# Keeping the last group's image in SBUF, from the adds of layer 2 to the output of layer 3

## The chip, the cores and the metric

The kernel runs on one core of one Trainium2 chip. The metric is device time in microseconds of that core, from the first to the last instruction of one execution, with what lies around it; the median of several executions is compared. Engines are named as in the profile: PE (TensorE), DVE (VectorE), ACT (ScalarE), POOL (GpSimd), SP (SyncE, which issues nearly all DMAs).

## What is computed

The input is 16 images of 32 channels of 128 x 128 in float32. Four layers follow each other, each of the form `x = x + f(groupnorm(x))`, where the norm runs over two channels of one image:

```python
x = x + _L0_conv_ref(_gn(x), W2, b2, W1, b1)     # recurrent layer, along one axis
x = x + _L1_conv_ref(_gn(x), weight)             # 8-bit adder layer, sums of |patch - w|
x = x + _L2_conv_ref(_gn(x), weights1)           # Hartley transform, 32 x 32 modes mixed
x = x + _L3_conv_ref(_gn(x), ...)                # five edge filters, then an encoder and decoder
```

The change lies in layers 2 and 3. Layer 3 applies five edge filters, normalises each filter's result, and runs conv1, pooling, conv2, pooling, conv3, pooling, conv4, and then three pairs of a 2 x 2 transposed convolution and a 3 x 3 convolution (deconv1 and conv5, deconv2 and conv6, deconv3 and conv7). Its result is `orig * y`, where `orig` is the normalised x, and the kernel's output is x plus that.

## The kernel before

`program` runs layer 0 (`stage0`), and then `rest` runs everything else. The 16 images are four groups of four; an image's 32 channels take one quarter of the 128 partitions, so that a group fills them (image, channel).

**Order of the work.** In `rest` the adder layer (`Differences.run`, L757, L760, L647) goes through the images one after the other. Beside it a generator, `After.work`, does layers 2 and 3 for groups 0 to 2 whose images are finished. It yields estimates of its PE work and of waits, and the class `Weave` uses these to decide after which adder instructions its steps are written down; a step that has to come later is put off with `weave.later(us, step)`. When the adder layer is over, group 2 is half done, and a copy of the generator, `end`, does group 3. `drain` then merges the two by their estimated clocks, and from there on only this order, and the compiler's own ordering of what is ready, sets each engine's queue. When group 2 is over, `weave.alone` is set, group 3 uses eight PSUM banks where it had four, and evictions alternate between DVE and ACT.

**Group 3's stages**, which are those of any group:

- `forward`: the transform, and the mixing of the modes.
- `back` (L1254 on): the mixed modes go back through two products (L1278, L1323). `residual` loads pieces of x2, the input of this layer, in 16 DMAs (L1257, 512 KB each), eight ahead. For each piece `take_out` adds the product to it (L1301) and takes `bn_stats` (L1303). The sum, x3, is stored to DRAM (L1307), after which the buffer is loaded again. Then the norm's mean and scale are worked out (`stats3`, `shift3` at L1341).
- `frames` (L1346 on): a ring of four buffers `xp` of 20 rows each, which is 16 rows and a halo of two rows above and below; a buffer has 132 columns. Half a buffer at a time, x3 is loaded (L1367, up to 640 KB), normalised in place by ACT (L1373) with its mirrored border columns copied (L1379, L1380), and stored to DRAM as `xn` with its borders (L1392).
- `statistics`: the mean and variance of the five filters' results, from products of every image row with itself and the next two (L1428), summed with tables on DVE (L1492). Behind the ring, later pieces are loaded 2 us, and normalised 18 us, after a half has been read; at the end the ring is filled again from `xn` (L1397).
- The filters are folded into conv1's 5 x 5 weights `wf` (L1557, L1559) and border terms (L1719), and `conv1` (L1745) reads the ring, which is again loaded from `xn`. conv2 follows.
- `small_layers`: conv3, conv4 (L1595), and the pairs up5 and up6. A pair of transposed convolution and convolution is one set of 2 x 2 products for each of the four positions in an output cell (`Composed.round`, L905, with border terms at L930). After up6, `spread` writes each 32 partitions of PSUM apart (L1683 on DVE, L1686 on ACT) into y6, an image of 66 x 66 for each (image, channel).
- `last`: the pair up7 in 16 rounds, eight pairs of them, four units of 32 rows. Here PSUM's partitions are (quarter of the unit's rows, output channel) and the bank is the image. xr is loaded from `xn` in that layout (16 DMAs of 528 KB, L1814; group 3 has buffers for all four units). The means and scales are brought to this layout by a product (L1826), each pair of rounds is taken out by four DVE operations (L1874, `(acc + one) * v`), and each unit gets four ACT operations that add the mean (L1844) and 16 stores of 128 KB (L1853).

Of the kernel before, what the change touches and what calls it, by code (L numbers as in the profile page):

```python
# [7 lines left out]
F32 = mybir.dt.float32  # L8
# [8 lines left out]
HW = H * W  # L17
# [475 lines left out]
def rest(nc, tc, cst, sel16, bias, m1, r1, a, d, out):  # L493


    with ExitStack() as ctx:
        sm = ctx.enter_context(tc.tile_pool(name="s1_sm", bufs=1))
        stat = sm.tile([128, B, 8, 6], F32, name="stat2")
        with tc.tile_pool(name="s1_ps0", bufs=2, space=PSUM) as ps:
            first = Differences(nc, sm, ps, cst, sel16, m1, r1, a["adder_w"], d, stat)  # L500
        bg = ctx.enter_context(tc.tile_pool(name="b_ps", bufs=4, space=PSUM))
        after = After(nc, tc, "left", sm, bg, cst, bias, a, d, stat, out)
        weave = after.weave = Weave(after.work(range(NG - 1)))
        start = len(nc.cur_bb.bb.instructions)
        with ExitStack() as front:
            first.run(tc, front, weave)
        keep_order(nc, tc, start)

        end = copy.copy(after)
        end.side, end.ps = "right", ctx.enter_context(tc.tile_pool(name="c_ps", bufs=4, space=PSUM))  # L510
        end.spare = bg

        end.buffers = {"t_x": 8, "xm": 8, "xw": 4, "t_w": 6, "t_r": 8, "frames": 4, "gm": 5, "e_v": 6, "l_x": 4}
        end.weave = Weave(end.work([NG - 1]))
        end.weave.now = end.weave.base = weave.now
        end.weave.finished = B - 1
        drain(weave, end.weave)
# [315 lines left out]
class Composed:  # L833
# [59 lines left out]

    def round(self, src, n, acc, pick):

# [3 lines left out]
        for tap in range(4):  # L899
            for j in range(4):  # L900
                par, row, rows, o = pick(j)
                top, left = row + par // 2 + tap // 2, par % 2 + tap % 2
                for blk in range(4):
                    part = slice(32 * blk, 32 * blk + 32)
                    nc.tensor.matmul(  # L905
                        acc[blk][32 * j : 32 * j + 32, o : o + rows * n],
                        t[part, 4 * par + tap, :],
                        src[part, top : top + rows, left : left + n],
                        start=tap == 0,
                        stop=tap == 3,  # L910
                        skip_group_check=True,
                    )
            yield rows * n / 512 * 0.2 + 0.95
            if tap != 2:
                continue
            for j in range(4):
                par, row, rows, o = pick(j)
                pr, pc = par // 2, par % 2
# [7 lines left out]
                for k, to, width in parts:  # L926
                    for blk in range(4):
                        part = slice(32 * blk, 32 * blk + 32)
                        b = self.bd[part]
                        nc.tensor.matmul(  # L930
                            acc[blk][32 * j : 32 * j + 32, to],
                            t[part, 16 + k, :],
                            bass.AP(b.tensor, b.offset, [list(b.ap[0]), [0, width]]),
                            start=False,
                            stop=False,
                            skip_group_check=True,
                        )
# [21 lines left out]
class After:  # L959


    def __init__(self, nc, tc, side, sm, ps, cst, bias, a, d, stat, out):
        self.nc, self.tc, self.side, self.ps, self.cst, self.bias = nc, tc, side, ps, cst, bias
        self.a, self.d, self.stat, self.out = a, d, stat, out
        self.spare, self.banks = None, 0
        self.sm, self.scales = sm, {}
# [9 lines left out]
    def work(self, groups):  # L976
        if 0 in groups:
            yield from self.prepare()
        for g in groups:
            with self.pool("g_sm") as sm:  # L980
# [6 lines left out]
                with ExitStack() as kept:  # L987
                    yield from self.encoder(g, kept)
                    yield from self.last(g, g + 1 if g + 1 in groups else None)

# [250 lines left out]
    def back(self, g, load):  # L1241
# [6 lines left out]
        with self.pool("t_z") as zp_, self.pool("t_r", ahead) as rp:  # L1248
# [6 lines left out]
            def residual(n):  # L1255
                xr.append(rp.tile([128, 2, 4 * W], F32, name="xr2"))
                nc.sync.dma_start(xr[n], rows(n)(x2))  # L1257

            xr = []
            stat = zp_.tile([128, 32, 6], F32, name="stat3")  # L1260
            zi = zp_.tile([128, 32, 32], F32, name="zi")
            for blk in range(4):
# [3 lines left out]
                )  # L1266
            for n in range(ahead):
                residual(n)
            yield -12.0
# [26 lines left out]
            def take_out(n, pf):  # L1296
                while ready.get(n):
                    weave.done(ready[n])
                for r in range(2):
                    v = xr[n][:, r]  # L1300
                    nc.vector.scalar_tensor_tensor(v, pf[r], 2.0**-15, v, ALU.mult, ALU.add)  # L1301
                for r in range(2):
                    nc.vector.bn_stats(stat[:, 2 * n + r, :], xr[n][:, r])  # L1303
                weave.dve += 2.8

                def store():
# [29 lines left out]
            take_out(*previous)  # L1336
            weave.later(7.0, lambda: [load(ch, half) for ch in range(self.buffers["frames"]) for half in range(2)])
            mv = zp_.tile([128, 1, 2], F32, name="mv3")
# [4 lines left out]
            )  # L1343
            yield -2.5

    def frames(self, g, pool):  # L1346
# [54 lines left out]
    def statistics(self, g, pool, frames, sides, out, tables):  # L1401
# [9 lines left out]
        ahead = self.buffers["frames"]  # L1411
        ready = {(n // 2, n % 2): normalise(n // 2, n % 2, 0.5 + 4.0 * n) for n in range(2 * ahead)}
        tables_ahead = self.buffers["gm"]
# [23 lines left out]
        for ch in range(H // 16):  # L1437
# [3 lines left out]
            for l in range(2, 18):  # L1441
                if l == 8:
                    yield ("done", ready[ch, 1])
                    store(ch, 1)
                r = 16 * ch + l - 2
                own = [r2 for r2 in (r, r + 1) if (r, r2) in GRAM_AT]
# [16 lines left out]
                if (ch, half) in ((0, 0), (H // 16 - 1, 1)):  # L1463
# [3 lines left out]
                    for k, cols in enumerate(ends):  # L1467
                        nc.vector.tensor_copy(c[:, :, 2 * k : 2 * k + 2], xp[:, rows, cols])
                weave.dve += 0.3

                def following(ch=ch, half=half):
# [45 lines left out]
    def encoder(self, g, kept):  # L1517


        nc, tc, cst, weave, bias = self.nc, self.tc, self.cst, self.weave, self.bias  # L1520
        y2 = self.padded(kept.enter_context(self.pool("e_y2")), 32, "y2")
        with self.pool("e_in") as xp:
            frames = self.frames(g, xp)
            yield from self.back(g, frames[0])
            with self.pool("e_f") as fp:
                yield from self.first_layers(g, fp, frames, y2)
# [44 lines left out]
    def small_layers(self, cp, rp, y1, y2):  # L1571
# [3 lines left out]
        if not y1:  # L1575
# [3 lines left out]
            y3, y4, y5 = (self.padded(cp, n, f"y{i}") for n, i in ((16, 3), (16, 4), (32, 5)))  # L1579
            self.y6 = y6 = self.padded(rp, 64, "y6")  # L1580
            yield -7.0
# [48 lines left out]
        def upsampled(src, n, up, dst):  # L1630

            rows = min(n, 512 // n)
            for r in range(0, n, rows):
# [15 lines left out]
                yield -2.0 if n == 16 else -4.5  # L1649

        if y1:
            yield from conv(y1, 64, "conv2", pool_into(y2, 64, 1))
            return
        yield from conv(y2, 32, "conv3", pool_into(y3, 32, 2))
        yield from conv(y3, 16, "conv4", flat)
        yield from upsampled(y4, 16, up5, y5)
        yield from upsampled(y5, 32, up6, y6)

# [17 lines left out]
    def spread(self, dst, src, blk, b, engine):  # L1676

        nc, weave = self.nc, self.weave
        for j in range(4):
# [5 lines left out]
            else:  # L1685
                nc.scalar.activation(d, s, AF.Identity, bias=bj)  # L1686
                weave.act += 0.45

    def conv1(self, g, pool, frames, y1, sides, wf, b1):
# [107 lines left out]
        for v in spreads:  # L1797
            weave.done(v)

    def last(self, g, following_group):  # L1800
# [252 lines left out]
```

## Time and profile before

| what | us |
|---|---|
| median of 3 runs (lowest, highest) | 6654.82 (6647.18, 6657.32) |
| the profiled execution | 6630.3 |
| its span, first to last instruction | 6628.4 |
| PE busy, DVE busy, ACT busy | 5329.5, 5552.5, 5436.8 |
| DMA read and written in HBM | 510.69 MB and 200.00 MB |
| largest group: ACT d_act, L757 | 4428.8 in 626 instructions |
| second: DVE d_dve, L760 | 3871.9 in 1678 |
| the chain that ended last, by engine | PE 32%, issue 29%, DVE 20%, ACT 14%, DMA 3% |

A profile line of a group names the line of the kernel, the engine, the operation, what it writes and reads with shapes, the count, busy us and mean ns, and the idle time of the engine ahead of it with what ended it. "issue" is idle time for which the profile shows no wait. A busy PE is not a PE at its peak, since matmuls overlap; therefore the prediction also looks at how many of them a stretch holds. The granted clock is a share of the full TensorE clock.

### The profile page before, as it was taken

The page shows a single profiled execution, that of the slowest core. Times are in us where ns is not written, and L with a number is a line of the kernel's source. Part 1 is how long each engine was busy: PE and PEld are TensorE (multiplying, and loading weights), DVE is VectorE, ACT ScalarE, POOL GpSimd, SP SyncE. Part 2 cuts the span into 40 slices and gives each one's busy share as a digit, 9 for nine tenths or more (in the row PEclk, how much of TensorE's full clock was granted, in tenths as well). Part 3 has the DMA queues.
Part 4 walks back from the last instruction along what each step waited for, and adds up shares of the span by engine and source line. Part 5 has one row for each costly group of instructions (what it writes and reads, how often), then busy time and mean ns, then how long its engine had stood idle before and what let it go on. Part 6 is the DMA issues. An engine that isn't in the chain of part 4 may idle for free.

```text
span 6628.4 us, 269240 instructions
## 1 busy us (share of the span) xinstructions
PE 5329.5 (80%) x126168; PEld 2776.6 (42%) x126168; DVE 5552.5 (84%) x6858; ACT 5436.8 (82%) x3191; POOL 69.9 (1%) x67
## 2 busy tenths in 40 slices
PE   3698677787777879997887879998877879887896
PEld 3676233333334433333333433333333433454584
DVE  7898899999999989998999999999999998242322
ACT  3898899999999999998999989999999998102112
POOL 0000000000000000000000000000000000000000
PEclk9999899999988989998989889999998889988897
DMA  7553322121254632212553732221553642347304
GB/s 317 213 189 116 79 55 62 53 53 45 67 146 114 196 92 72 57 45 52 123 150 97 216 110 61 56 55 43 133 147 90 196 122 76 115 136 216 94 27 108
DMA packets 380767, 728.06 MB, mean 110 GB/s; under 512 B 73284, under 2 KB 225348, under 8 KB 368772
## 3 DMA queue, kind: packets, MB, share of 16 engines
q1 hardware_dynamic: 372180, 676.41, 35.7%
q0 software_dynamic: 7040, 33.80, 1.5%
q8 instruction: 987, 16.17, 1.0%
q14 instruction: 128, 1.05, 0.1%
q10 hardware_dynamic: 432, 0.64, 0.0%
HBM read 510.69 MB, written 200.00 MB: 107 GB/s over the span
## 4 chain that ended last, share of the span: by engine, by line
PE 32%; issue 29%; DVE 20%; ACT 14%; DMA 3%; SPq 1%; POOL 0%; DVEq 0%; ACTq 0%; POOLq 0%
DVE d_dve L760 12%; PE acc L1745 11%; ACT d_act L757 10%; PE acc L647 9%; PE pg L223 3%; PE acc L905 3%; PE acc L1595 2%; PE acc L1428 2%; ACT gt L237 2%; DVE y L1683 1%; ACT junk L198 1%; DVE stat L124 1%; DMA x_in<-in_x_dram 1%; ACT th L247 1%; DVE pooled L1672 1%
## 5 line engine op out<-in xcount | busy, mean ns | idle before, releaser
L757 ACT ACTIVATE d_act<-q,neg 128x8192 f16<-128x8192 f16 (+1 forms) x626 | 4428.8, 7151 | 152.5 <-PE acc L647 125.7
L760 DVE TENSOR_SCALAR d_dve<-q,qw 128x8192 f16<-128x8192 f16 (+1 forms) x1678 | 3871.9, 2362 | 168.8 <-PE acc L647 149.2
L647 PE MATMUL acc<-d_dve,sel 128*32 128x512 f16 x26848 | 1873.4, 402 | 441.7 <-DVE d_dve L760 375.9
L647 PEld LDWEIGHTS <-sel 128*32 128x32 f16 x36864 | 1002.0, 100 | 2084.2 <-issue 1413.5
L1745 PE MATMUL acc<-xp,wf 32*32 32x512 f32 x25600 | 971.3, 607 | 19.0 <-issue 15.6
L647 PE MATMUL acc<-d_act,sel 128*32 128x512 f16 x10016 | 727.2, 412 | 311.5 <-ACT d_act L757 298.4
L1745 PEld LDWEIGHTS acc<-xp,wf 32*32 32x32 f32 x25600 | 420.9, 103 | 368.9 <-issue 287.5
L1686 ACT ACTIVATE y<-pooled,b 32x128 f32<-32x128 f32 x456 | 182.3, 400 | 427.8 <-DVE pooled L1672 421.7
L677 PE MATMUL acc<-q,zero 128*32 128x512 f16 x5676 | 406.5, 398 | 0.8 <-issue 0.8
L905 PE MATMUL acc<-y,u_conv 32*32 32x256 f32 (+1 forms) x9728 | 342.4, 469 | 77.3 <-issue 59.5
L223 PE MATMUL pg<-h,wb 64*64 64x20 f32 (+15 forms) x8192 | 342.4, 306 | 59.4 <-DVE h L251 33.0
L237 ACT ACTIVATE gt<-pg,bias 128x20 f32<-128x20 f32 (+15 forms) x1024 | 332.5, 384 | 41.5 <-PE pg L223 39.3
L223 PEld LDWEIGHTS pg<-h,wb 64*64 64x64 f32 x8192 | 252.5, 151 | 133.9 <-DVE h L251 79.5
L1428 PE MATMUL acc<-xp 32*64 32x204 f32 (+3 forms) x8576 | 252.9, 345 | 62.0 <-issue 61.7
L905 PEld LDWEIGHTS acc<-y,u_conv 32*32 32x32 f32 x9728 | 155.1, 111 | 205.0 <-issue 158.0
L1844 ACT ACTIVATE xr<-xr,l_ms 128x1024 f32<-128x1024 f32 x64 | 68.8, 1147 | 208.7 <-DVE xr L1874 158.8
L1428 PEld LDWEIGHTS acc<-xp 32*64 32x64 f32 (+1 forms) x8576 | 172.1, 134 | 152.9 <-issue 147.0
L677 PEld LDWEIGHTS <-zero 128*32 128x32 f16 x5676 | 169.4, 101 | 156.0 <-issue 30.5
L1780 DVE TENSOR_TENSOR acc<-acc,cut 128x4 f32<-128x4 f32 x256 | 36.3, 165 | 233.0 <-PE acc L1745 230.4
L1373 ACT ACTIVATE xp<-xp,shift,stats 128x1280 f32<-128x1280 f32 (+1 forms) x64 | 91.4, 1433 | 162.6 <-DVE shift L1341 111.6
L1874 DVE SCALAR_TENSOR_TENSOR xr<-acc,l_one,xr 128x512 f32<-128x512 f32 x128 | 87.6, 743 | 155.0 <-PE acc L905 134.7
L223 PE MATMUL pg<-xn,wb 64*64 64x2 f32 (+63 forms) x4096 | 185.5, 291 | 27.1 <-issue 18.8
(217 smaller groups left out, 3748.1 us busy)
## 6 DMA issues: line engine op xcount, KB each, us to landing
q<-q_d SPq DMA_DIRECT2D x128, 536.2 KB, 9.8
xp<-xn_d SPq DMA_DIRECT2D x64, 660.0 KB, 5.0
xp<-x_d SPq DMA_DIRECT2D x56, 640.0 KB, 6.4
xr<-xn_d SPq DMA_DIRECT2D x64, 528.0 KB, 11.9
x_in<-in_x_dram SPq DMA_DIRECT2D x16, 2048.0 KB, 14.7
xn<-in_xs_dram SPq DMA_DIRECT2D x64, 512.0 KB, 7.1
res<-in_x_dram SPq DMA_DIRECT2D x64, 512.0 KB, 8.9
x_d<-res SPq DMA_DIRECT2D x64, 512.0 KB, 5.1
```

The source lines that it names most:

```text
L223: nc.tensor.matmul(bank[c][q][64 * pair : 64 * pair + 64, :, :width], wb[half, 4 * kind + KIND[q]].rearrange("p b o -> p (b o)"), v[half], ...
L237: nc.scalar.activation(gt[:, q, :, :n], bank[c][q][:, :, :n], AF.Tanh if q == G else AF.Sigmoid, bias=bias[:, KIND[q] : KIND[q] + 1],)
L647: self.nc.tensor.matmul(acc[k][32 * j : 32 * j + 32, :], self.sel16[:, i // 9, :], d[:, row : row + 4, c : c + W], start=first, stop=last,)
L677: self.nc.tensor.matmul(acc[k][32 * j : 32 * j + 32, :], self.zero, q[:, :4, :W], start=False, stop=False)
L757: nc.scalar.activation(dst, src, AF.Relu, bias=self.neg[:, i : i + 1])
L760: nc.vector.tensor_scalar(dst, src, self.qw[:, i : i + 1], 0.0, ALU.subtract, ALU.max)
L905: nc.tensor.matmul(acc[blk][32 * j : 32 * j + 32, o : o + rows * n], t[part, 4 * par + tap, :], src[part, top : top + rows, left : left + ...
L1373: nc.scalar.activation(v, v, AF.Identity, bias=self.shift3, scale=self.stats3[:, 1])
L1428: nc.tensor.matmul(gram[blk][j : j + width, at : at + n], xp[part, l, 2 + j : 2 + j + width], xp[part, rows, j : j + width + 4], start=sta ...
L1595: nc.tensor.matmul(acc[blk][32 * j : 32 * j + 32, : rows * n], wc[name][part, tap, :], src[part, at : at + rows, kw : kw + n], start=tap == 0,
L1686: nc.scalar.activation(d, s, AF.Identity, bias=bj)
L1745: nc.tensor.matmul(acc[blk][32 * j : 32 * j + 32, :], tap_of("all", tap)[rows], xp[rows, 4 * j + kh : 4 * j + kh + 4, kw : kw + W], start= ...
```

## The change

Only group 3 takes the new way (`end.whole = True`); groups 0 to 2 keep the old one.

- One tile `image` of 128 x 132 x 132 floats is made ahead of `back`. x2 is loaded into it by 16 DMAs of eight rows each, all issued at once. `take_out` adds in it and takes its statistics from it; x3 is neither stored nor loaded.
- All 16 normalising steps work in it, put off by 0.5 + 1.5 n us, and nothing is stored or loaded again; a chunk of 20 rows is a view of it. Ahead of a chunk's row 16 the statistics now wait for the next chunk's first half, since the halo is shared. conv1 reads the same views.
- up6 writes y6 as four quarters of 16 rows with one halo row above and below: the partitions are (quarter, channel), and the image is a free dimension. For this its rounds take all quarters of the rows at once, with half the columns in a product and twice the products; each bank is taken out by one operation of 128 partitions, and six copies fill the halo rows between quarters.
- In the last rounds a bank is therefore a quarter of the rows, and its partitions are (image, channel), as in `image`. up7 is multiplied into `image` in place, the mean is added in place, and four DMAs of 512 KB for each unit store the output. The loads of `xn` and the product for the means are gone.

```diff
-        end.spare = bg
+        end.spare, end.whole = bg, True
...
-    def round(self, src, n, acc, pick):
+    def round(self, src, n, acc, pick, quarter=0):
...
+                    par, row, rows, o = pick(blk if quarter else j)
+                    top, left = row + par // 2 + tap // 2 - quarter * blk, par % 2 + tap % 2
                     part = slice(32 * blk, 32 * blk + 32)
+                    own = src[part, j] if quarter else src[part]
...
+            if self.whole:
+                for row in [32 * i + 8 * k for k in range(4) for i in range(4)]:
+                    src = bass.AP(x2.tensor, x2.offset + g * 4 * CHW + row * W, [[HW, 128], [W, 8], [1, W]])
+                    nc.sync.dma_start(self.image[:, 2 + row : 10 + row, 2 : W + 2], src)
+            else:
+                for n in range(ahead):
+                    residual(n)
...
+                    v, p = xr[n][:, r] if not self.whole else in_place(n, r), pf[r]
+                    if self.whole:
+                        p = p.rearrange("p (r w) -> p r w", w=W)
+                    nc.vector.scalar_tensor_tensor(v, p, 2.0**-15, v, ALU.mult, ALU.add)
...
+                if self.whole:
+                    return
...
+    def kept_image(self, pool):
...
+        self.image = t = pool.tile([128, PW, PW], F32, name="image")
...
+                v = t[:, row : row + 8, 2 : W + 2]
+                nc.scalar.activation(v, v, AF.Identity, bias=self.shift3, scale=self.stats3[:, 1])
...
+                nc.scalar.copy(t[:, lo:hi, 1], t[:, lo:hi, 3])
+                nc.scalar.copy(t[:, lo:hi, W + 2], t[:, lo:hi, W])
...
+        nothing = lambda ch, half: None
+        return nothing, normalise, nothing, nothing, lambda ch: t[:, 16 * ch : 16 * ch + 20, :]
...
+        if self.whole:
+            ready = {(n // 2, n % 2): normalise(n // 2, n % 2, 0.5 + 1.5 * n) for n in range(H // 8)}
...
+                if l == 16 and self.whole and ch + 1 < H // 16:
+                    yield ("done", ready[ch + 1, 0])
...
+        def to_quarters(src, n, up, dst):
...
+            for pr in range(2):
+                acc = [self.acc() for _ in range(4)]
+                for pc in range(2):
+                    yield from up.round(src, n, acc, lambda j: (2 * pr + pc, rows * j, rows, 256 * pc))
+                yield SUMMED
+                for blk in range(4):
+                    self.evict(
...
+            self.neighbours(dst, 2 * rows)
...
-        yield from upsampled(y5, 32, up6, y6)
+        yield from (to_quarters if self.whole else upsampled)(y5, 32, up6, y6)
...
+    def neighbours(self, t, n, above=True, below=True):
...
+        for q in range(3):
+            a, b = t[32 * q : 32 * q + 32], t[32 * q + 32 : 32 * q + 64]
+            if above:
+                self.nc.vector.tensor_copy(b[:, :, 0, 1 : w - 1], a[:, :, n, 1 : w - 1])
+            if below:
+                self.nc.vector.tensor_copy(a[:, :, n + 1, 1 : w - 1], b[:, :, 1, 1 : w - 1])
...
+    def last_in_place(self, g):
...
+            for unit in range(4):
+                for pr in range(2):
+                    acc = [self.acc() for _ in range(4)]
+                    for pc in range(2):
+                        pick = lambda q: (2 * pr + pc, 16 * q + 4 * unit, 4, 256 * pc)
+                        yield from up.round(self.y6, 64, acc, pick, 16)
+                    yield SUMMED
+                    for q in range(4):
+                        first = 2 + 32 * q + 8 * unit + pr
+                        v = x[:, first : first + 7 : 2, 2 : W + 2].rearrange("p r (w b) -> p r w b", b=2)
+                        nc.vector.scalar_tensor_tensor(
+                            v, acc[q].rearrange("p (b r w) -> p r w b", b=2, w=64), one, v, ALU.add, ALU.mult
+                        )
+                    yield -2.5
+                for q in range(4):
+                    row = 32 * q + 8 * unit
+                    v = x[:, 2 + row : 10 + row, 2 : W + 2]
+                    nc.scalar.activation(v, v, AF.Identity, bias=self.stats3[:, 0])
+                    to = self.out.offset + g * 4 * CHW + row * W
+                    nc.sync.dma_start(bass.AP(self.out.tensor, to, [[HW, 128], [W, 8], [1, W]]), v)
```

## The prediction

> **What bounds the kernel now.** I read the page's 40 slices first, to see where the change can act at all.
>
> ```profile
> PE   3698677787777879997887879998877879887896
> DVE  7898899999999989998999999999999998242322
> ACT  3898899999999999998999989999999998102112
> ```
>
> The last line of columns matters: for 34 slices (to about 5640 us) VectorE and ScalarE are full, the adder layer's loop sets the time, and the diff touches nothing there. In the last six slices both are nearly idle: this is the tail, where groups 2 and 3 finish side by side and then group 3 alone. All of the change lies there. Next I asked for the tail stage by stage (columns: stage, length, busy us and counts of PE, weight loads, DVE, ACT, POOL, then granted clock, DMA share, GB/s).
>
> ```profile
> 5868.00:5966.00 98.00, 77.33 (x1750) 49.83 (x1750) 66.93 (x154) 6.39 (x16) 0.00 (x0) 0.71 0.57 175
> 6006.00:6136.00 130.00, 93.26 (x3194) 58.87 (x3193) 17.85 (x48) 24.50 (x37) 0.00 (x0) 0.88 0.73 187
> 6136.00:6204.00 68.00, 39.84 (x1608) 29.06 (x1612) 38.98 (x100) 4.30 (x4) 2.15 (x4) 0.60 0.45 121
> 6204.00:6443.00 239.00, 236.11 (x7482) 183.77 (x7465) 44.69 (x144) 34.21 (x72) 0.00 (x0) 0.98 0.15 44
> 6514.00:6560.00 46.00, 26.34 (x834) 17.22 (x836) 7.83 (x15) 4.08 (x5) 0.00 (x0) 0.58 0.89 184
> 6560.00:6614.00 54.00, 39.30 (x1818) 27.09 (x1791) 13.63 (x20) 10.21 (x10) 0.00 (x0) 0.94 0.50 119
> ```
>
> In order (counts are matmul records, two for each fp32 product): group 3's way back; its statistics beside group 2's last rounds; the folding of conv1's weights; conv1; the first and the second part of group 3's last rounds. Only conv1 is full of TensorE work. The last two rows are the same instructions, yet 834 matmuls took 46 us beside a DMA share of 0.89, and 1818 took 54 us beside 0.50. The PE's order of time in the statistics shows how it loses time (start, us, instructions, idle before):
>
> ```profile
> 6017.02 3.02 PE L1428 MATMUL acc<-xp 32*64 32x204 f32 x128 [0.95 <-issue]
> 6021.03 3.02 PE L1428 MATMUL acc<-xp 32*64 32x204 f32 x128 [1.00 <-issue]
> 6030.54 3.00 PE L1428 MATMUL acc<-xp 32*64 32x204 f32 x57 [6.49 <-issue]
> 6039.85 4.70 PE L1428 MATMUL acc<-xp 32*64 32x204 f32 x128 [3.92 <-issue]
> 6049.36 4.37 PE L1428 MATMUL acc<-xp 32*64 32x204 f32 x91 [4.80 <-issue]
> ```
>
> Runs of 128 matmuls with gaps that no semaphore explains. The page has 17.2 MB on its instruction queues (16.17 and 1.05) for 269240 instructions, 64 B each, and 987 packets on the first, 16.4 KB each: 256 instructions, which are 128 matmuls with their 128 weight loads. So a gap ends when the next packet of instructions lands, and it is 1 us when the DMA engines are quiet and 4 to 6.5 us when they are loaded. I measure by the packet: 130 us for 3194 matmuls are 5.21 us a packet, 54 us for 1818 are 3.80.
>
> Last, the waits of PE over the way back, and of the DMA queue over the last rounds:
>
> ```profile
> PE acc L1595 <- DMA w_conv<-in_conv_dram: 10.8, 1, 10.8
> PE acc L905 <- issue: 3.8, 2, 3.5
> ```
>
> The first is group 2's conv3, whose weights SP could not issue before 5922.25, behind reloads that waited for x3 stores to land.
>
> **The change part by part**, against the profiled execution (6630.3 us, its span 6628.4); lower is a gain.
>
> *Way back (5868 to 5987).* Removed: 16 stores of x3 (L1307, 512 KB), the reloads tied to them, and 16 loads of frames (L1367, 640 KB). The 16 image loads (512 KB) go out at once where now 8 do, at about 5812; at the 250 to 390 GB/s that the loads between 5810 and 5824 show, 8.4 MB take 22 to 34 us, and the first add comes at 5894: hidden; without that cover they would cost some 10 us. conv2's last eviction ends at 5920.1 and conv3 needs it, so conv3 restarts there instead of 5926.2: -6. Between 0 (the adds on DVE set the pace anyway, 67 of 98 us busy) and -11. The adds and bn_stats work on rows 132 apart instead of a solid block; the near row is the strided L1874, 744 ns against 683 for L1301: at most 32 x 0.06 = +2, taken as 0.
>
> *Normalising (ACT).* Sixteen steps of 1024 columns: 1.25 + 2 x 0.21 = 1.67 us, 27 us in all, now 30. They no longer wait for x_d (ACT waited 44.9 us for it). But they become ready together when the shift is ready (5986.5), and up to 9 more of them than now (7) may stand on ACT ahead of group 2's up6 evictions (8 x 0.73 us), for which PE waited 5.1 us already: 0 to +15. PE can take statistics instead, so I take the lower part, +5. The new halo wait (row 16 on the next chunk's first half) queues the remaining statistics behind it on PE; with steps of 1.67 us for 8 rows against 3.8 us of PE a packet (8 rows) it costs 0.
>
> *Statistics beside group 2 (6006 to 6136).* Removed: the store of xn (8.7 MB), the loads of x3 (7 MB) and of xn again (5.3 MB), 21 of the 44.8 MB moved between 5960 and 6210; also their places on SP, which group 2's loads and stores stood behind. The 23.8 MB left, over some 200 us, are 119 GB/s, the very figure of the 3.80 us row. 25.0 packets x (5.21 - 3.80) = -35. [...] Ends: 0, and -43 at 3.47 us a packet (5865.4 to 5868.9, DMA share 0.06).
>
> *Folding (6136 to 6204).* 37 us are DVE's chain (es_w, square root, wf), untouched. PE then idles 13.1 us in the 704 matmuls of L1719, with out stores beside it: -6, between 0 and -13.
>
> *conv1.* 236.1 of 239 busy: -2 (0 to -3).
>
> *up6 and the small layers (6443 to 6514).* up6 goes from 2 x 64 matmuls of 512 columns to 4 x 64 of 256, and with the border products from 384 to about 700 PE records, 5.5 packets: at 3.8 us 21 us, now 17 (6494 to 6511). Evictions shrink from 32 on 32 partitions (12.2 us on each engine) to 8 on 128 (two of about 0.7 us an engine after the second half), but six copies between quarters follow (near row: 32x256, 0.46 us, from PSUM; 0.2 to 0.46 each), and the next layer needs them. up7's weights still leave when up6's last matmul has read the pool, 4.5 us as now. Start of the last rounds: 6494 + 20.5 + 4.5 = 6519 against 6514.2: +4.5 (0 to +8). Removed besides: one product and three small DVE operations for the means, about 1 us, in that figure.
>
> *Last rounds (6514 to 6614).* Same matmuls, 2652, 20.7 packets. The 16 loads of xn (528 KB, 19.8 us to land) go; out's stores stay as in the 54 us row. 20.7 x 3.80 = 78.7 against 100: -21. [...]
>
> *Tail.* Four stores of 512 KB instead of 16 of 128 KB, whose issue took 0.42 us each after ACT's 4.3: -2.5 (0 to -4).
>
> Sum: -6 + 5 - 35 - 6 - 2 + 4.5 - 21 - 2.5 = **-63**. From 6630.3 to 6567 in the profiled execution. The median of the runs is 24.5 us longer than that execution; the same 63 off 6654.8 gives **6592**. What comes late next: in the statistics and last rounds still PE's packets; in the folding DVE.
>
> **The rivals.**
> 1. [...] Chance 0.16.
> 2. *The image is ordered as a whole*, so the change does not do what it says: each normalising step waits for the products before it. 16 x (1.67 + some 0.6 of hand-over) = +37: 6629. Against: now the last rounds read y6 from 6514.2 while its evictions run to 6515.7, so parts of a tile are told apart. Chance 0.04.
> 3. *All gains at their far end* (3.47 us a packet, no ACT backlog): -6 - 43 - 11 - 3 + 2 - 27 - 3 = -91, 6564. Chance 0.15.
> 4. *Slower*: with other ready times the PE queue takes group 2's last rounds ahead of the statistics. Then its chain ACT, store, reload stands bare twice: 32 us (6099.7 to about 6131) and 38 us (6153.5 to 6192), now covered by statistics and folding, plus the 2.7 us of adds each: +75, net +12 and, with +15 of ACT backlog for +5, +22: 6677. It decides once more than 63 us are uncovered. Against: the modelled delays of both generators hardly change. Chance 0.03.
>
> **How the numbers follow.** Likeliest 0.62: 6592, its own range 6570 to 6614. The range 6556 to 6630 takes in rivals 1 to 3 where they centre and leaves about 2 in 10 out. A measurement of this kernel tells about 0.2% (13 us) from no change: faster 0.94, same 0.03, slower 0.03.
>
> **What would show it.** Right: 5.2 us a packet falls to about 3.8 in the statistics; the last rounds run at one pace of about 9.5 us per pair from their start; no ACT wait for x_d; conv3's wait under 2 us; the last rounds begin 4 to 5 us later after up5 than now. Wrong: gaps of 4 us beside a DMA share under 0.5; L1428 waiting for ACT; PE waiting for group 2's evictions over 15 us.

## The result and the profile after

| | us |
|---|---|
| median before, in the same comparison (4 runs) | 6655.34 (6647.18 to 6657.32) |
| median after (4 runs) | 6609.77 (6607.96 to 6630.47) |
| ratio after to before, 95% interval | 0.9944 (0.9931 to 0.9956) |
| forecast | 6592 (6556 to 6630) |
| the profiled execution after, its span | 6607.96, 6606.2 |

The ratio is worth 37 us, with an interval of 29 to 46; the forecast was 63. (The two medians lie 46 us apart.) So the direction and the range hold, and the size is some 20 us short.

First, the stages of the tail in the kernel after, in the columns of the prediction's table: the way back, statistics beside group 2, folding, conv1, and the two parts of the last rounds.

```profile
5878.00:5974.00 96.00, 83.74 (x1878) 51.29 (x1878) 67.14 (x157) 6.40 (x16) 0.00 (x0) 0.72 0.05 14
6014.00:6126.00 112.00, 88.06 (x3172) 56.77 (x3159) 16.91 (x46) 18.99 (x36) 0.00 (x0) 0.90 0.39 84
6126.00:6196.00 70.00, 38.83 (x1566) 26.62 (x1568) 39.56 (x101) 4.30 (x4) 2.15 (x4) 0.60 0.41 108
6196.00:6439.00 243.00, 237.29 (x7615) 190.65 (x7600) 46.55 (x154) 34.50 (x73) 0.00 (x0) 0.99 0.09 21
6516.00:6560.00 44.00, 33.12 (x1543) 24.06 (x1547) 10.90 (x16) 8.59 (x8) 0.00 (x0) 0.91 0.27 77
6560.00:6594.00 34.00, 21.58 (x1094) 15.42 (x1084) 8.18 (x12) 4.29 (x4) 0.00 (x0) 1.00 0.33 95
```

The last rounds did what was forecast: their first 44 us now hold 1543 matmuls where 46 us held 834. The statistics did so only in part. 3172 matmuls are 24.8 packets, 112 us are 4.52 us a packet, and the forecast had 3.80, although the DMA share fell from 0.73 to 0.39, below that of the row which the 3.80 came from. PE's order of time there shows where the rest is:

```profile
6032.70 4.62 PE L1487 MATMUL acc<-image 32*64 32x204 f32 x128 [5.78 <-issue]
6042.21 3.00 PE L1487 MATMUL acc<-image 32*64 32x204 f32 x57 [4.88 <-issue]
```

The large gaps are still there, as long as before, but only two of them. They fall in the one stretch in which loads run, as the DMA slices of 6000 to 6127 show (3.2 us a slice):

```profile
DMA  0000000799999920000000000000006984599700
GB/s 20 0 0 0 5 5 5 201 206 211 198 214 213 204 60 5 5 5 5 5 5 0 5 5 5 5 5 0 5 5 159 217 194 106 121 207 217 146 5 0
```

The first burst is group 2's loads of `xn` (528 KB each, rows of 4.2 KB, 12.2 us to land), and both gaps lie in it. The second is half stores of `out` with rows of 512 bytes and half one more unit of loads; its largest gaps are 2.3 and 2.7 us. A mean of 0.39 over the stage hides that. Gaps of over 4 us beside a mean share under 0.5 are what the prediction had named as a sign against it.

Last, a wait that before did not have, and one that stayed (PE, 6436 to 6606):

```profile
PE acc L1661 <- DMA w_conv<-in_conv_dram: 7.9, 1, 7.9
...
PE acc L908 <- DMA u_conv<-up_d: 3.6, 1, 3.6
```

To compare executions I measure from a mark, the start of the store `z_d` that ends group 3's forward transform, since the same code ahead of it takes a different time in each execution: it came at 5802.5 us in the profile of before, and at 5812.7 in that of after. Stage lengths in us, with a second profiled execution of the kernel after:

| from, to | before | after | after, again |
|---|---|---|---|
| mark to first statistics matmul | 190.3 | 188.0 | 191.2 |
| statistics, first to last matmul | 143.0 | 126.0 | 124.1 |
| to conv1's first matmul (folding) | 69.2 | 72.1 | 70.2 |
| conv1 | 238.9 | 238.1 | 236.2 |
| to the arrival of up7's weights | 70.3 | 79.2 | 79.3 |
| to the start of the last products into the output | 100.1 | 78.0 | 80.2 |
| to the end | 14.1 | 12.1 | 12.1 |
| mark to end | 825.9 | 793.5 | 793.3 |

The statistics and the last rounds, before and then after:

```profile
5992.80:6135.80 143.00, 100.19 (x3341) 61.35 (x3344) 25.22 (x68) 37.18 (x62) 0.00 (x0) 0.87 0.73 195
6514.20:6614.30 100.10, 65.92 (x2626) 44.26 (x2626) 21.28 (x34) 14.10 (x14) 0.00 (x0) 0.77 0.67 148
```

```profile
6000.70:6126.70 126.00, 95.69 (x3353) 59.96 (x3337) 24.15 (x63) 32.14 (x57) 0.00 (x0) 0.87 0.35 75
6515.90:6593.90 78.00, 54.60 (x2621) 39.48 (x2622) 19.08 (x28) 12.88 (x12) 0.00 (x0) 0.95 0.29 85
```

The tail is 32.5 us shorter. That is within the interval of the ratio; the 5 us up to its middle would have to lie ahead of the mark, where I can't locate them. The profiled execution of before was a quick one, 17 us below the fastest of the other runs, so its early mark says nothing of the change.

### The profile page after: what moved, and what is told of

Its sections match the earlier page's. It is cut to its first block, busy times and chain, and to the rows that moved or that the text cites. A ratio compares the mean times of both kernels' runs of the same rounds, so it can differ in the third digit from the quotient of the medians.

```text
span 6606.2 us, 269623 instructions
## 1 busy us (share of the span) xinstructions
PE 5331.0 (81%) x126486; PEld 2789.1 (42%) x126486; DVE 5543.3 (84%) x6844; ACT 5422.6 (82%) x3179; POOL 70.0 (1%) x67
## 4 chain that ended last, share of the span: by engine, by line
issue 33%; PE 29%; DVE 18%; ACT 15%; DMA 4%; SPq 1%; POOL 0%; DVEq 0%; ACTq 0%; POOLq 0%
PE acc L1863 11%; DVE d_dve L760 11%; ACT d_act L757 10%; PE acc L647 8%; PE pg L223 3%; PE acc L908 2%; PE acc L1661 2%; ACT gt L237 2%; DVE y L1768 1%; ACT junk L198 1%; DVE stat L124 1%; DMA xm_d<-xm 1%; DMA x_in<-in_x_dram 1%; DVE pooled L1757 1%; DMA v<-fold_d 1%
## 5 line engine op out<-in xcount | busy, mean ns | idle before, releaser
L1863 PE MATMUL acc<-xp,wf 32*32 32x512 f32 x19200 | 757.3, 614 | 16.1 <-issue 12.9
L1771 ACT ACTIVATE y<-pooled,b 32x128 f32<-32x128 f32 x456 | 182.4, 400 | 429.9 <-DVE pooled L1757 423.7
L1863 PEld LDWEIGHTS acc<-xp,wf 32*32 32x32 f32 x19200 | 257.1, 104 | 324.9 <-issue 277.3
L1863 PE MATMUL acc<-image,wf 32*32 32x512 f32 x6400 | 218.7, 599 | 0.6 <-issue 0.4
L223 PE MATMUL pg<-xn,wb 64*64 64x2 f32 (+63 forms) x4096 | 186.9, 293 | 25.5 <-issue 17.2
L1661 PE MATMUL acc<-y,w_conv 32*32 32x512 f32 (+2 forms) x4608 | 172.2, 528 | 37.0 <-issue 18.5
L1487 PE MATMUL acc<-xp 32*64 32x204 f32 (+2 forms) x6432 | 180.1, 337 | 26.1 <-issue 26.0
L1994 ACT ACTIVATE xr<-xr,l_ms 128x1024 f32<-128x1024 f32 x48 | 51.6, 1147 | 164.8 <-DVE xr L2024 110.8
L1863 PEld LDWEIGHTS acc<-image,wf 32*32 32x32 f32 x6400 | 169.7, 103 | 37.9 <-issue 8.7
```

Source lines behind the costliest of these rows:

```text
L223: nc.tensor.matmul(bank[c][q][64 * pair : 64 * pair + 64, :, :width], wb[half, 4 * kind + KIND[q]].rearrange("p b o -> p (b o)"), v[half], ...
L1487: nc.tensor.matmul(gram[blk][j : j + width, at : at + n], xp[part, l, 2 + j : 2 + j + width], xp[part, rows, j : j + width + 4], start=sta ...
L1661: nc.tensor.matmul(acc[blk][32 * j : 32 * j + 32, : rows * n], wc[name][part, tap, :], src[part, at : at + rows, kw : kw + n], start=tap == 0,
L1863: nc.tensor.matmul(acc[blk][32 * j : 32 * j + 32, :], tap_of("all", tap)[rows], xp[rows, 4 * j + kh : 4 * j + kh + 4, kw : kw + W], start= ...
```

## The experiments

**Theory**: PE's packets of instructions come late while loads with long rows are in flight; the mean of bytes or share over a stage doesn't tell. **Rivals**: any bytes delay packets, whatever their form; or the gain of the last rounds comes from the layout (products in place, quarter images) and not from the loads that went. Beside this, two waits for weights took back some of the gain.

**The kernel after, again.** No edit.

> The changed kernel once more, unaltered, as the control for the other runs on the same chip. Counted from the z store that ends group 3's forward part, the tail took 826 us before and 793 us after; if that is the whole effect, this run's tail is again 793 +- 3 us, and the ratio to the kernel before is 0.995 (33 of 6650 us), whatever the first 5800 us do. If the adder layer's part is changed too (it began the tail 6 us later in the first profile), the start of the tail is again late by some 6 us.

6610.02 (6603.08 to 6619.99), ratio 0.9942 (0.9930 to 0.9955), tail 793.3 us. The stages repeat within 3.2 us (table above): differences below that prove nothing here.

**The kernel before, with earlier loads.** Three of the four units of `xn` are asked for in conv1, ahead of the last rounds.

> The kernel before, with no image kept, but with the loads of xn for three of the four last units issued during conv1 (buffers: three units, six residuals, four filter tables). Theory (the loads in the last rounds held up PE's instruction packets): the last rounds fall from 100 us to about 80, all of the in-place version's gain there. Rival (the gain came from the new layout, or from the clock): they stay at 95 to 100 us. Total by the theory about -18 us against before, 0 to +5 us by the rival.

```diff
+            if self.early and ch == 1:
+                self.xr_early = [self.load_last(g, unit, self.xr_pool) for unit in range(self.buffers["l_x"])]
...
-        end.buffers = {..., "t_r": 8, ..., "e_v": 6, "l_x": 4}
+        end.buffers = {..., "t_r": 6, ..., "e_v": 4, "l_x": 3}
```

6655.18, ratio 1.0008 (1.0001 to 1.0014). Statistics and last rounds:

```profile
6011.00:6177.00 166.00, 110.24 (x3351) 68.95 (x3337) 25.25 (x67) 37.33 (x62) 0.00 (x0) 0.79 0.81 205
6559.80:6644.80 85.00, 59.13 (x2626) 40.64 (x2626) 22.12 (x37) 14.89 (x15) 0.00 (x0) 0.89 0.44 104
```

The last rounds fell from 100.1 to 85.0 with the old layout: so at least 15 of the 22 us are the loads. But SP did not issue them in conv1. They stood ready as soon as the normalised rows were stored and went out among the statistics (24 loads of 528 KB there, against 12), and the statistics grew from 143.0 to 166.0. The same bytes cost as much in the other place, or more; the fewer buffers may have a part in that.

**The kernel after, group 2's loads of the tail in short rows.**

> The changed kernel, with group 2's loads of xn (the only ones left beside group 3's statistics) cut into runs of 512 bytes, the same useful bytes in four times as many DMAs. Theory A (an instruction packet waits behind transfers with long rows, 4 KB each): the gaps of 5 to 9 us in the statistics fall to 1 to 2 us, the 112 us stage to about 98, total -12 to -15 us against the changed kernel. Rival B (any busy DMA engine holds packets up, by the bytes or the share): nothing is gained, within 3 us, or it is slower by the longer issue of the loads.

```diff
+                    if weave.draining:
+                        for blk in range(4):
+                            rows = bass.AP(t.tensor, first + 32 * blk * PADDED + 2, [[PADDED, 32], [PW, 8], [1, W]])
+                            nc.sync.dma_start(inner(xr)[32 * j : 32 * j + 32, blk], rows)
+                        continue
```

6605.26 (6599.16 to 6607.51), ratio 0.9931 (0.9918 to 0.9943). Tail 782.3, statistics:

```profile
6007.60:6125.80 118.20, 93.59 (x3353) 59.27 (x3337) 24.08 (x62) 32.14 (x57) 0.00 (x0) 0.91 0.48 78
```

126.0 became 118.2, at a higher DMA share; the largest gap during the loads is 2.65 us instead of 5.78. So here the form of a load counted, not its bytes alone. But packets of instructions still came late, 4.8 to 5.8 us apart.

**The kernel after, group 3's late weights early.** Those of conv3, conv4 and the three pairs are loaded at the start of the group's layer 3, in memory of their own.

> The changed kernel, with group 3's weights of conv3, conv4, up5, up6 and up7 loaded ahead of its way back into a pool of their own, so that no load waits for memory to come free. Theory (new waits behind the pools' memory took back part of the gain): PE's waits for conv3's weights (7.9 us) and up7's (3.6 us) go, and -8 to -10 us against the changed kernel follow. Rival (conv2's evictions and the copies between quarters set those times anyway): -3 us or less.

```diff
+        if g in (NG - 1,):
+            wp = kept.enter_context(self.pool("e_w"))
+            self.soon = {n: replicated(nc, wp, self.a[n], 9, f"w_{n}") for n in ("conv3", "conv4")}
+            self.soon["up"] = [up.loaded(wp) for up in (self.up5, self.up6, self.up7)]
```

6611.5, ratio 0.9948 (0.9934 to 0.9962). Both waits for weights are gone, and from conv1's end to the last rounds it is 72.3 us instead of 79.2. But the first statistics matmul came 194.6 us after the mark instead of 188.0 to 191.2, and the program did not become faster.

**The kernel after, with loads put back into the last rounds.** 16 loads whose data nothing uses, solid rows of 4 KB in the one kernel (width W), rows of 512 bytes in the other (width PW, so that rows lie apart).

> The changed kernel with 16 loads added at the start of the last rounds, 512 KB each, rows of 4 KB written to solid places of memory, their data unused (8.4 MB; the kernel before loads 8.65 MB there in 16 loads of 528 KB). Everything else as in the changed kernel, whose last rounds took 78 us from the arrival of up7's weights to the last image product, against 100 before. Theory (loads with long rows in flight hold up the 16.4 KB packets of PE's instructions): gaps of 4 to 7 us come back while the loads are in flight, the last rounds take 93 to 102 us, the program 15 to 22 us more than the changed one. Rival (the layout of the quarter images and the products in place, or the clock, brought the 22 us): 78 to 82 us, no more than 4 us of difference.

> The same 16 added loads of 512 KB, unused, but written to rows of 132 elements, so that each row of 128 moves by itself (512 bytes at a time). Theory (row length decides): at most a third of what the solid loads cost, last rounds of 80 to 86 us, the program 2 to 8 us above the changed kernel. Rival (bytes or the engines' busy share decide): as much as the solid loads, or more, since the short rows keep the DMA engines busy longer: 93 us or more. The first short-row run (statistics 8 us shorter with the third group's loads cut) speaks for the theory, but with a tail of gaps left.

```diff
+            for k in range(16):
+                more = yp.tile([128, 8, W], F32, name="more", bufs=16)
+                src = bass.AP(x2.tensor, x2.offset + 8 * k * W, [[HW, 128], [W, 8], [1, W]])
+                nc.sync.dma_start(more[:, :, :W], src)
```

Ratios 0.9947 (0.9932 to 0.9962) and 0.9949 (0.9935 to 0.9962). The last rounds, solid and then in rows:

```profile
6527.60:6614.90 87.30, 60.00 (x2621) 43.19 (x2622) 19.09 (x28) 12.90 (x12) 0.00 (x0) 0.83 0.50 169
```

```profile
6521.30:6611.10 89.80, 64.49 (x2621) 46.17 (x2622) 19.09 (x28) 12.88 (x12) 0.00 (x0) 0.78 0.60 166
```

87.3 and 89.8 us, against 78.0: the loads cost 9 and 12 us, too near each other to be told apart. The solid rows fell between theory and rival: 8.4 MB of them cost less than half of what the 8.65 MB before did. The short rows were not cheaper, so the theory missed there. The ratios are worth 2 to 5 us more than after, within their intervals, though the profiled tails are 9 and 10 us longer than after.

**The kernel before, its last loads in short rows.** The same edit as in the changed kernel, for groups 2 and 3.

> The kernel before, with nothing of the change; only the loads of the image for the last rounds in the tail (16 of the third and 16 of the last group, 528 KB each with rows of 4.2 KB) are cut into four each, of 128 rows times 8 pieces of 512 bytes. Theory (row length decides): the last rounds fall from 100 to 82 to 90 us and the statistics from 143 to 132 to 139 us, the program is 15 to 28 us shorter than before, so that a good half of what the change brings comes without it. Rival (bytes decide, or the change's gain is in its layout): within 5 us of the kernel before; the four times as many issues on SP could even cost some us.

6638.55 (14 runs), ratio 0.9982 (0.9973 to 0.9990). Last rounds:

```profile
6523.00:6617.10 94.10, 69.58 (x2626) 46.22 (x2626) 21.19 (x35) 13.97 (x14) 0.00 (x0) 0.74 0.90 156
```

PE's idle time in the stage (length less busy) fell from 34.2 to 24.5 us, nearly that of the kernel after (23.4). But PE's busy time rose from 65.9 to 69.6, at a granted clock of 0.74 instead of 0.77. Statistics 144.3: no gain. The tail as a whole is 1.3 us shorter in this profile, and it does not show where the 12 us of the ratio lie. So shorter gaps were not enough, and row length as the one cause falls.

**What replaced it.** In the trace of before, each of the 35 gaps of PE on "issue" of over 0.6 us in the statistics and the last rounds ends 1.3 to 1.6 us after a packet has landed: these gaps are waits for packets. The trace has each packet of the instruction queue q8 (16,384 bytes). It takes 1.0 to 1.4 us on average in each of these stages, loads or not. What differs is how far apart the packets start while loads fly; I read the load rate from the DMA slices:

```
loads in the last rounds              rate      loads last   packets start apart   last rounds
none (after)                                                 3.4 to 3.5 us, some 6  78.0
4.2 KB rows, 32 partitions (before)   214 GB/s  39 us        9.1 to 9.5             100.1
512 B rows, 32 partitions             181       46           4.9 to 6.1             94.1
4 KB rows, 128 partitions             402       21           6.2, 6.4, once 8.8     87.3
512 B rows, 128 partitions            290       30           4.1 to 6.3, once 7.4   89.8
```

So here a load cost its duration times the share of packets that would have started in that time and did not. 39 us x (1 - 3.5/9.2) = 24, 46 x (1 - 3.5/5.5) = 17, 21 x (1 - 3.5/6.3) = 9, 30 x (1 - 3.5/5.3) = 10; measured against the kernel after: 22, 16, 9 and 12. Both sides come from the same traces, so this sums them up and is no separate test. Short rows cut a packet's delay from 5.7 to 2.0 us, but the loads last longer (46 us instead of 39). I had taken the first factor for the whole.

**Short rows and early weights together**, in the kernel after.

> The changed kernel with both edits tried alone before: the third group's image loads in the tail cut to rows of 512 bytes (alone: 6605.3, the stretch from the last group's first store of moments to the end 782.3 us against 793.5), and the last group's weights of conv3, conv4 and the three upsampling layers loaded early (alone: 6611.5, that stretch 788.4). If their gains add, that stretch is 776 to 779 us and the program 6598 to 6603 us. If the earlier weights only move a wait (they lost 6 us ahead of the first normalisation that the removed waits gave back), it is 782 or more and the program stays at 6605.

6605.15, ratio 0.9927 (0.9915 to 0.9940). The tail is 778.7 us, as if the gains added, yet the time stays at that of the short rows alone. A difference of 4 us in one profiled tail is about what the stages vary by.

**Wide loads.** Each load writes one of the four image blocks on all 128 partitions, where it wrote four blocks on 32. Bytes, count and row length stay. First in the kernel before:

> The kernel before, with nothing of the change; each unit's four loads of the image for the last rounds still have 528 KB and rows of 4.2 KB each, but each now writes one block of all 128 partitions (before: all four blocks of 32 partitions). In the runs so far the spacing of PE's instruction packets while loads fly, times the loads' duration, gave the cost: 9.2 us apart for the 36 us of the last group's loads at 214 GB/s into 32 partitions at a time; 6.3 us apart for 21 us at 402 GB/s into 128 partitions (unused solid loads); 5.2 us apart, but for 46 us at 181 GB/s, with rows of 512 bytes; 3.5 us in quiet. Theory (packets are fetched at longer intervals for as long as loads fly; the loads' rate decides with the row length): loads at 330 to 400 GB/s for 22 to 27 us, packets 6 to 7 us apart, the last rounds 86 to 91 us instead of 100, the statistics 128 to 138 instead of 143, the program 12 to 25 us less than before. Rival (only bytes decide, or the layout of the added loads made them cheap): within 5 us of before.

```diff
-                for j in range(4):
-                    first = t.offset + g * 128 * PADDED + (2 + 32 * unit + 8 * j) * PW
-                    rows = bass.AP(t.tensor, first, [[PADDED, 32], [32 * PADDED, 4], [1, 8 * PW]])
-                    nc.sync.dma_start(xr[32 * j : 32 * j + 32], rows)
+                for blk in range(4):
+                    first = t.offset + (g * 128 + 32 * blk) * PADDED + (2 + 32 * unit) * PW
+                    rows = bass.AP(t.tensor, first, [[8 * PW, 4], [PADDED, 32], [1, 8 * PW]])
+                    nc.sync.dma_start(xr[:, blk], rows)
```

6682.76, ratio 1.0072 (1.0059 to 1.0085): slower, where I had expected 12 to 25 us less. I had expected a higher rate and got 108 GB/s at a DMA share of 0.2 to 0.3, as if a load ran on about four of the sixteen engines (an estimate: 0.2 to 0.3 of sixteen are 3.2 to 4.8). The first dimension of its access pattern has four entries; no run shows whether that is why. Its last rounds, and DVE's waits in them:

```profile
6561.30:6645.20 83.90, 61.62 (x2626) 42.88 (x2626) 22.23 (x36) 15.00 (x15) 0.00 (x0) 0.83 0.31 116
```

```profile
DVE xr L1874 <- DMA xr<-xn_d: 37.6, 11, 4.4
```

All 8.65 MB fly through this stage, nearly to its end, and yet no gap of PE on "issue" is over 1.4 us, and the packets start 3.4 to 4.1 us apart but for five times, one of 8.1 and four of 5.1 to 5.8 us. The stage is 16 us shorter than before although DVE now waits for the loads. But SP was held by these loads for 67.5 us, and the stores of `out` were issued only behind them:

```profile
6558.51 67.52 SPq L1814 DMA_DIRECT2D xr<-xn_d  x16
6626.14 50.89 SPq L1853 DMA_DIRECT2D out_dram<-xr  x64
```

The end behind the stage took 35 us instead of 14, more than the stage had gained, and the missing stores may have a part in its short gaps. The program lost most in the statistics, which took 175.7 us. There ACT waited for loads of the ring that stood in the same queue (28.8 us for one half, 18.4 for the next); DVE waited for ACT, and PE stood for 38.8 us behind DVE:

```profile
6071.41 1.47 ACT L1373 ACTIVATE xp<-xp,shift,stats 128x1280 f32<-128x1280 f32 x1 [28.84 <-DMA xp<-x_d]
```

In the kernel after, in all groups:

> The changed kernel with the same wide form of the loads that are left to it (groups 0 to 2; group 2's lie in the tail). Theory: group 2's loads land in half the time (12 to 13 us now), packets 6 to 7 us apart for 11 us instead of 9 us apart for 23 us, the statistics 116 to 120 us instead of 124 to 126, the second loads in the folding cost 2 to 3 us less; the program at 6596 to 6604 us, no worse than the short rows (6605.3). Rival (bytes decide): 6607 to 6612, as the changed kernel.

6585.68, ratio 0.9932 (0.9920 to 0.9945) on a chip with before at 6633.93. The statistics fell to 105.5 us and the tail to 762.4, 31 us less than after. But beside the adder layer the slow loads held up others. ScalarE's wait there, in the kernel after and in this one:

```profile
ACT xq L594 <- DMA xq<-x_d: 12.9, 4, 10.4
```

```profile
ACT xq L594 <- DMA xq<-x_d: 39.5, 6, 20.8
```

27 us more of waiting on ScalarE, which has little to spare there (busy for 5269 of the first 5640 us of the kernel after), for 31 gained in the tail. That calls for the wide form in the tail alone (in the code: where `weave.draining` holds).

> The changed kernel with the form of the load that writes one block of 128 partitions (which in the two last runs moved 108 GB/s on a busy share of 0.2, and left PE's instruction packets at 3.5 to 4 us) only in the tail, that is for group 2's last loads; the loads beside the adder layer stay as they were. In the run with that form everywhere the tail from the last group's first store of moments was 762.4 us against 793.5, the statistics 105.5 against 126; but the adder layer lost some 27 us, since ScalarE waited 39.5 us for xq's loads instead of 12.9. Theory (packets wait for the DMA engines that loads occupy, and loads on a few of the engines leave the others free; the loss in the front is the slow loads in the queue ahead of xq's): both hold apart, the tail 760 to 766 us, no loss in the front, 0.988 to 0.990 of the kernel before (6570 to 6585 us by the chip). Rival (the shorter statistics are only work that the front had not left over, a shift of the boundary): the tail back at 785 or more, ratio 0.993 to 0.994.

6591.4 (6588.22 to 6608.77) with before at 6656.3, ratio **0.9908 (0.9894 to 0.9921)**: faster than both kernels. The wait for xq is 13.0 us again, the tail 771.7 us, so the gain is no shift of the boundary; it is 6 us less than forecast, 5 of them ahead of the first statistics matmul. Statistics and their DMA slices:

```profile
6007.30:6115.00 107.70, 89.95 (x3341) 55.86 (x3344) 24.08 (x62) 31.42 (x57) 0.00 (x0) 0.97 0.24 77
```

```profile
DMA  0000000062222222222222221000000878702222
GB/s 8 0 0 0 6 0 6 6 174 78 98 111 106 111 109 106 111 112 111 103 112 111 105 112 55 6 0 6 6 6 19 208 170 219 176 3 70 98 102 112
```

The same megabytes as in the kernel after, at half the rate for twice the time; the packets start 3.5 to 4.1 us apart all along them; the clock is 0.97 instead of 0.87, and the stage is 18 us shorter.

With the early weights added:

> The same with the last group's weights of conv3, conv4 and the three upsampling layers loaded early as well. Alone the early weights took away waits of 7.9 and 3.6 us and gave 6 us back ahead of the first normalisation; with the short rows they brought nothing more. If that loss belongs to the earlier issue of the weights themselves, this run is within 3 us of the one without; if it was chance of one execution, 6 to 10 us faster, 0.987 to 0.989 of before.

6594.77, ratio 0.9908 (0.9894 to 0.9921): the same. Again the waits are gone and the first statistics matmul is 5.4 us later (195.5 against 190.1). So it is the early loading that costs this, not chance: the first statistics matmul came 194.3 to 195.5 us after the mark in the three kernels with it, and 187.2 to 191.2 us in six executions without it. The traces show what it delays. SP issues these weights ahead of the loads of `z_d`, which leave 12.1 to 13.0 us after the mark instead of 6.4 to 6.9, and the first product of the way back, which reads them, starts at 17.6 to 20.1 us instead of 14.0 to 14.3.

## Why the prediction was right in direction and too large

- *Last rounds, -21*: measured -22.1 and -19.9. Right, and for the reason given. PE's idle time there fell by 10.8 us and its busy time by 11.3, from 65.9 to 54.6 for the same matmuls, while the granted clock rose from 0.77 to 0.95. Busy time times clock is 51 and 52 us, so half of the gain is the clock (8.5 of 19.9 us in the second execution, with 57.5 us at 0.90). The forecast has no term for the clock; its row of 3.80 us, at a clock of 0.94, had it in unsaid. The trace of before has the clock at 1.0 or at 0.5, in stretches of multiples of 3.4 us, and at 0.5 for 34 us on end from 709 us after the mark, with PE busy for 17.2 of them, where the packets came late. With the short rows in the kernel before, PE was busy for 74% of the last rounds at a clock of 0.74, in the kernel after for 70% at 0.95: what decides the clock, no run here shows.
- *Statistics, -35, with +5 for ACT's order*: -17.0 and -18.9 together. The failed term is "the 23.8 MB left, over some 200 us, are 119 GB/s, the very figure of the 3.80 us row". Here the mean bytes over a stage did not set a packet's wait; what flew at that moment did, and in what form. The 3.80 us row had stores in rows of 512 bytes, and the statistics kept group 2's loads in rows of 4.2 KB. With these loads in the wide form the stage fell from 143.0 to 107.7, by 35, or from 5.5 to 4.1 us a packet: the forecast was the size of a stage without late packets. The +5 did not appear: PE's wait for ACT ahead of up6 is 5.17 us, 5.11 before. No run shows the forecast's end of 0 for this stage: the kernel after took 17.0 and 18.9 us less.
- *Folding, -6*: +2.9 and +1.0. Same cause: group 2's second loads give a gap of 8.8 us in L1837 (6.9 before). With short rows the folding took 67.2, with wide loads in the tail 64.6.
- *Way back, -6*: -2.3 and +0.9. The wait that I had named did go: PE waited 10.8 us for the weights of group 2's conv3, and now 0.5 (the line below). From the first add to the first statistics matmul it is 92.0 and 92.4 us instead of 98.1, the 6 us of the forecast. But the first add came 3.8 and 6.6 us later after the mark. The failed term is "hidden": I had put the 16 image loads, all issued at once, at nothing. They fly from 10 to 43 us after the mark, beside the first product. In that time the packets start 4.4 to 6.3 us apart, where before they were 3.7 to 3.9 apart but for two (8.3 and 5.1). The same 34 us, before and after, hold 1019 and 925 matmuls (853 in the second execution). This is read from the traces; no run leaves these loads out:

```profile
PE acc L1661 <- DMA w_conv<-in_conv_dram: 0.5, 1, 0.5
```

```profile
5812.50:5846.50 34.00, 28.12 (x1019) 16.10 (x1003) 3.37 (x12) 6.40 (x16) 0.00 (x0) 1.00 0.41 131
5822.70:5856.70 34.00, 28.82 (x925) 15.51 (x918) 3.37 (x12) 6.39 (x16) 0.00 (x0) 0.90 1.02 256
```

- *up6 and small layers, +4.5*: +8.9. From up5's eviction to the last rounds it is +3.7, near the forecast. What I missed is the new 7.9 us for conv3's weights: before, their memory came free at conv1's end, and now only after conv2's evictions (the last is ACT's, L1771).
- *conv1 -2, tail -2.5*: -0.8 and -2.7; -2.0.
- *Late packets*: they take some 1.1 us, and yet PE stood for up to 6.5 us in the statistics of before until the next. Rival 1, that group 2's own traffic keeps the gaps, was right for the statistics (5.78 and 4.88 us stayed) and wrong for the last rounds (78.0 us); it gave 6626. Its sum of -29 lies nearer to the tail's -32.5 than my -63 does.

## What to carry to other kernels

Where TensorE runs many small matmuls in straight code, look for gaps on "issue" and hold them against the DMA slices of that very moment, not against a stage's mean. A load that fills all DMA engines (a DMA share of 1.0) was dear here for as long as it flew (22 us in the last rounds), also where no wait for it showed (4 to 7 us in the way back); a slower one, at a DMA share of 0.2, was the better one, but only where nothing urgent queued behind it. And for a load that starts late, ask which of its two conditions comes last, the queue or the memory.

## What the runs showed of the hardware

- A load of 528 KB with the same rows moved at 214 GB/s when it wrote 32 partitions x 4 blocks, and at 108 GB/s and a DMA share of 0.2 when it wrote 128 partitions through an access pattern whose first dimension is 4.
- 512 KB loads into 128 partitions moved at 402 GB/s with solid 4 KB rows and at 290 with 512-byte rows.
- Instruction packets of 16,384 bytes took 1.0 to 1.4 us on average beside any of these loads; it is their start that moved, from 3.4 to up to 9.5 us apart. PE, when it had stood on "issue", went on 1.3 to 1.6 us after one had landed (before).
- Open: whether the wide loads spare PE because they leave its packets' engine free, or because of their low rate. The rates do not order the other four forms (214 GB/s gave 9.2 us, 402 gave 6.3), which speaks for the first; no run separates them.
